# Expert attention: query, key and value projections as matmuls of 256 columns, and the PSUM tiles of the stage regrouped

## The chip, the core and the metric

The kernel runs on one core of a Trainium2 chip. A core has a matrix engine (PE, with its weight loads listed apart as PEld), a vector engine (DVE), a scalar engine (ACT), GpSimd (POOL) and an engine that issues DMAs (SP). Each runs its own queue of instructions in order; they wait for each other through semaphores. PE writes its results to PSUM, a small memory of eight banks of 512 float32 per partition; DVE and ACT read it from there. The metric is the time of one execution in device microseconds (us).

Before the change the median of 3 runs is 2612.46 us (2608.49 to 2620.51).

## The reference

A small vision model on 128 images, everything in float32: a tokenizer of two convolutions gives each image 64 tokens of 256 features; layer 0 has an attention with a ReLU distance, and then "expert attention"; layer 1 has a linear attention and a routed mixture of experts. The change is in expert attention alone. What that computes, cut to its core:

```python
xn = (x - mean) / sqrt(var + EPS) * norm_w
gate = softmax(xn @ router_w.T + router_b)             # 4 experts per token
xc = xn.reshape(B, T, C, DC)                           # C = 4 slices of DC = 64 features
qkv = einsum('btcd,ekd->btcek', xc, qkv_w)             # per slice and expert: q, k, v
q, k, v = ...                                          # H = 2 heads of 32 each
attn = softmax(einsum('bcehtd,bcehsd->bcehts', q, k) * scale)
y = einsum('bcehts,bcehsd->bcehtd', attn, v)
y = einsum('btced,eod->btceo', y, proj_w) + proj_b     # per expert
out = einsum('btceo,bte->btco', y, gate).reshape(B, T, D)
return residual + out @ out_w.T
```

An image has 64 tokens, so there are, for each image, 4 slices x 4 experts x 2 heads = 32 score matrices of 64 x 64.

## The kernel before

The stages follow each other: tokenizer (to 190 us in the trace), ReLU attention (to about 1085 us), expert attention (1085 to about 1824 us), then linear attention, routing and experts. In expert attention two images are worked on together, a **pair**, because 2 x 64 tokens fill the 128 partitions; there are 64 pairs, and four pairs form a block that shares statistics, transposes and gates. The order of work on every engine is written out by hand (`tc.manual_schedule()`): each engine executes its instructions in the order in which the Python code makes them. The framework puts in the semaphores, and gives each PSUM tile a slot of its pool; a slot is handed on when all who used its last tile are done.

`rest` (L1289) is the loop over pairs. One turn p works on three pairs at once: the scores and softmax of `cur` (pair p), the mixing of `old` (p-1), the output of `older` (p-2), and the projections of `new` (p+1). In order:

1. `cur.scores` (L1055, matmul L1064): 64 matmuls of 32 rows x 64 columns into two PSUM tiles of two banks (pool `fps`, tag `sc`). Then DVE: `maxima` (L1074) and `less_max` (L1078), two each.
2. `old.transposes` (L1100) and `transposed` (L1105): 16 transposes of the attention weights into four PSUM tiles of one bank (`pt`), each copied to SBUF by ACT.
3. Work for a later block (`do((p, "PE"))` and so on): in turns p%4 = 0 and 1 transposes of its normalised rows (`ptx`, L936, copied by ACT in L941), in p%4 = 2 the router's logits (L956), in p%4 = 3 the gates' softmax: DVE L976 to L978, ACT L981, DVE L984 and L985.
4. `older.output` (L1131, PSUM tile `po`), `old.mixed` (L1115, 32 matmuls, PSUM tile `pz`).
5. ACT: `cur.exponents` (L1081), two. DVE: `sums(0)` (L1084, L1085), then `older.added` (L1135), which adds `po` to the residual. POOL: `weights` (L1091, L1092).
6. ACT: `old.mixed_copied` (L1126), which copies `pz`.
7. `new.queries_keys(fc)` (L1004, matmul L1019), for the two halves fc of the features: 16 matmuls of 64 rows x 128 columns into a tile of tag `sc`, and after each half two copies by ACT (`queries_keys_copied`, L1025).
8. DVE: `cur.sums(1)`; POOL: `cur.weights(1)`.
9. `new.values(h)` for h = 1 and 0 (L1027, matmul L1039): 16 matmuls each, into two PSUM tiles of one bank (`pv`). `values_kept(h)` (L1047) takes them out: for h = 1 DVE adds the bias (L1053, two instructions), for h = 0 ACT copies (L1051, two).
10. `do((p, "DVE"))`: in turns p%4 = 1 and 2 statistics of later rows (L868, L869).

A float32 matmul is two MATMUL and two LDWEIGHTS rows in the trace, a transpose one of each. `pt`, `ptx`, `po`, `pz` and `pv` all come from one pool of four single banks (`apq`, tag `pq`, function `ps`, L303 to L306), in turn; the two tiles of tag `sc` take the other four banks.

Of the kernel before, what the change touches and what calls it, by code (L numbers as in the profile page):

```python
# [12 lines left out]
F32 = mybir.dt.float32  # L13
# [7 lines left out]
P = 128  # L21
# [38 lines left out]
def bcast(ap, axis, n):  # L60

    v = ap.unsqueeze(axis)
    shape = list(v.shape)
    shape[axis] = n
    return v.to_broadcast(shape)
# [225 lines left out]
class Shared:  # L291
# [3 lines left out]
    def __init__(self, c, ctx, end):  # L295
        def pool(name, bufs, ctx=ctx, **k):
            return ctx.enter_context(c.tc.tile_pool(name=name, bufs=bufs, **k))

        self.np_, self.bp, self.small = pool("an", 2), pool("ab", 2), pool("as", 1)

        self.atp, self.ep = (pool(n, k, end, side="right") for n, k in (("aat", 1), ("ae", 2)))
        self.end = end
        self.psq = pool("apq", 4, space=PSUM)  # L303

    def ps(self, shape, name):
        return self.psq.tile(shape, F32, tag="pq", name=name)  # L306
# [455 lines left out]
def expert_attention(c, sh, front, hd, normw, wr, br, wqkv, wvT, wproj, bproj, wout):  # L762
# [5 lines left out]
    SCALE = float(1.0 / np.sqrt(np.float32(32)))  # L768
    NP = B // 2
    NB = 4  # L770
    ps, small = sh.ps, sh.small
    nw = small.tile([P, 2], F32, name="nw")
    nc.sync.dma_start(nw, normw)
    wrs = small.tile([P, 2, 4], F32, name="wrs")
# [215 lines left out]
    class Pair:  # L990
# [10 lines left out]
            qk = ring(sh.bp, "k", [P, 2, 16, T])  # L1001
            self.qk = qk.rearrange("p (c a e t) -> p c a e t", c=4, a=2, e=2)

        def queries_keys(self, fc, among_scores=False):  # L1004

            if among_scores:
                pq = self.pools.pss.tile([P, 2, 2, 2, P], F32, tag="sc", name="pqk")
                pq = [pq[:, par] for par in range(2)]
            else:
                pq = [ps([P, 2, 2, P], "pqk") for _ in range(2)]  # L1010
            self.pq[fc] = pq
            for k in range(2):
                for eh in range(2):
                    for half in range(2):
                        o = slice(half * 64, half * 64 + 64)
                        for par in range(2):
                            r = slice(par * 64, par * 64 + 64)
                            f = k * D + eh * P + half * 64
                            nc.tensor.matmul(  # L1019
                                pq[par][o, k, eh, :], wt.w[r, f : f + 64], self.xT[r, fc], start=True, stop=True  # L1020
                            )

        def queries_keys_copied(self, fc, copy=nc.scalar.copy, pars=range(2)):
            for par in pars:
                copy(self.qk[:, 2 * fc + par], self.pq[fc][par])  # L1025

        def values(self, h):  # L1027

# [65 lines left out]
        def transposes(self, x, h):  # L1094

            e = self.e[x]
            self.pt[x, h] = pt = ps([P, 4, P], "pt")
            for cq in range(4):
                i = h * 8 + cq * 2
                nc.tensor.transpose(pt[:, cq, :], e[:, i : i + 2, :].rearrange("p e s -> p (e s)"), c.ident)  # L1100

        def transposed(self, x, h):
            if h == 0:
                self.pT[x] = self.pools.ep.tile([P, 2, 4, P], F32, tag="pT", name="pT")
            nc.scalar.copy(self.pT[x][:, h], self.pt.pop((x, h)))  # L1105

        def mixed(self):

            pz = ps([P, 2, P], "pz")
            for fc in range(2):  # L1110
                for j in range(2):
                    t = slice(j * 64, j * 64 + 64)
                    for r in range(4):
                        for par in range(2):
                            nc.tensor.matmul(  # L1115
                                pz[par * 64 : par * 64 + 64, fc, t],
                                self.v[:, par, r % 2, 2 * fc + j, r // 2 * 64 : r // 2 * 64 + 64],
                                self.pT[r // 2][:, r % 2, 2 * fc + par, t],
                                start=(r == 0),
                                stop=(r == 3),  # L1120
                            )
            self.pz = pz
# [3 lines left out]
            nc.scalar.copy(self.z, self.pz)  # L1126

        def output(self):
            self.po = po = ps([P, D], "po")
            for fc in range(2):  # L1130
                nc.tensor.matmul(po, self.z[:, fc], wt.o[:, fc, :], start=(fc == 0), stop=(fc == 1))  # L1131

# [56 lines left out]
    def do(key):  # L1189
        for step in work.pop(key, ()):  # L1190
            step()
# [46 lines left out]
    def first(cur, new, chunk, last):  # L1238

        new.queries_keys(0)  # L1240
        chunk.exponents()
        new.queries_keys_copied(0)
        chunk.sums()
        chunk.weights()
        cur.scores()
        cur.maxima(0)
        cur.less_max(0)
        y.normal_scalar(0)
        new.queries_keys(1)
        cur.maxima(1)  # L1250
        cur.less_max(1)
        chunk.transpose()
        new.queries_keys_copied(1)
        chunk.transposed()
        cur.exponents(0)
        last.outcome(0)
        last.outcome(1)
        for par in range(2):
            last.outcome_copied(0, par)
        cur.sums(0)  # L1260
        cur.weights(0)
        cur.exponents(1)
        for par in range(2):
            last.outcome_copied(1, par, nc.vector.tensor_copy)
        cur.sums(1)
        cur.weights(1)
        new.values(0)
        new.values_kept(0)
        last.back(0)
        last.back(1)  # L1270
        last.added(0)
        last.added(1)
        for k in range(1, 4):
            y.normal_scalar(k)
        new.values(1)
        new.values_kept(1)
        last.back(2)
        last.back(3)
        last.added(2)
        last.added(3)  # L1280
        sh.end.close()
        front.open()
        for k in range(NB):
            x.stream(k)
        do((0, "POOL"))
        do((0, "PE"))
        do((0, "ACT"))

    def rest(chunk, last):  # L1289
        with (  # L1290
            tc.tile_pool(name="fe", bufs=4) as ep,
            tc.tile_pool(name="fps", bufs=2, space=PSUM) as pss,
            tc.manual_schedule(),
        ):
            Pair.pools = SimpleNamespace(ep=ep, pss=pss)
            older, old, cur = None, None, pairs[0]
            for p in range(NP):
                new = Pair(p + 1, blocks[(p + 1) // NB]) if p + 1 < NP else None
                if p == 0:
                    first(cur, new, chunk, last)  # L1300
                    old, cur = cur, new
                    continue
                if p == 8:
                    front.weights()
                cur.scores()
                for x in range(2):
                    cur.maxima(x)
                for x in range(2):
                    cur.less_max(x)
                for x in range(2):  # L1310
                    for h in range(2):
                        old.transposes(x, h)
                        old.transposed(x, h)
                do((p, "PE"))
                do((p, "ACT"))
                do((p, "DVE0"))
                if older:
                    older.output()
                old.mixed()
                cur.exponents(0)  # L1320
                cur.exponents(1)
                do((p, "ACT1"))
                do((p, "DVE1"))
                do((p, "POOL0"))
                cur.sums(0)
                cur.weights(0)
                if older:
                    older.added()
                old.mixed_copied()
                if new:  # L1330
                    for fc in range(2):
                        new.queries_keys(fc, True)
                        new.queries_keys_copied(fc)
                else:
                    c.busy(ps([P, 2 * D], "idle"), wt.w, 3)
                do((p, "ACT2"))
                cur.sums(1)
                cur.weights(1, nc.gpsimd if new else nc.vector)
                do((p, "POOL"))
                if new:  # L1340
                    for h in (1, 0):
                        new.values(h)
                        new.values_kept(h)
                do((p, "DVE"))
                older, old, cur = old, cur, new
            for x in range(2):
                for h in range(2):
                    old.transposes(x, h)
                    old.transposed(x, h)
            older.output()  # L1350
            old.mixed()
            old.mixed_copied()
            older.added()
            old.output()
            old.added()
        assert not work
# [1004 lines left out]
```

## Time and profile before

| | us |
|---|---|
| median of 3 runs | 2612.46 |
| the profiled execution's own time | 2610.73 |
| its span in the trace, first to last instruction | 2609.0 |
| expert attention's scores, start of pair 1's to start of pair 63's | 702.8 (62 turns, 11.34 each) |

Busy time in stretches of that stage, in us:

| stretch | PE | DVE | ACT | POOL |
|---|---|---|---|---|
| 1100 to 1200 | 95.67 | 86.55 | 71.72 | 70.71 |
| 1400 to 1500 | 97.79 | 88.27 | 72.07 | 66.25 |
| 1600 to 1700 | 93.15 | 83.14 | 68.61 | 64.59 |

The granted clock of the matrix engine is 0.98 to 1.00 of full speed in these stretches. In the profile's lines a name such as `kr<-pqk` means that the instruction writes tile `kr` and reads `pqk`; several SBUF tiles have names of the buffers that they reuse (`kr` holds queries and keys, `vr` values, `xnr`, `xTr` and `oTr` normalised rows and weights). "x64" counts rows merged into one line; the time is from the first's start to the last's end. In square brackets stands how long the engine had been idle before, and which instruction's end released it.

### The profile page before, as it was taken

How to read it: one execution, taken by the hardware profiler on the slowest of the kernel's cores; microseconds unless marked ns; L12 is line 12 of the kernel's file. 1: busy time of each engine (PE TensorE's matmuls, PEld its weight loads, DVE VectorE, ACT ScalarE, POOL GpSimd, SP SyncE). 2: the span in 40 equal slices, each digit the busy share in tenths (PEclk: the TensorE clock that was granted, in tenths of full speed). 3: DMA queues.
4: the chain of work that ended last, by engine and by line, in shares of the span. 5: the costliest groups of instructions: out<-in, count | busy, mean ns of one | idle time of the engine just before them, and what ended most of it. 6: DMA issues, size and time to landing. Idle time of an engine off the chain costs nothing. (4 is left out here: it accounts for less than half of the span.)

```text
span 2609.0 us, 86024 instructions
## 1 busy us (share of the span) xinstructions
PE 2474.7 (95%) x37681; PEld 1702.5 (65%) x37681; DVE 2011.4 (77%) x3000; ACT 1635.0 (63%) x3421; POOL 1625.8 (62%) x1428
## 2 busy tenths in 40 slices
PE   8989999999999999899999999999999968999997
PEld 4554444444444444588888888887566557888886
DVE  5759999999999999888888888877567785444443
ACT  2228899898898888776667776675444533223232
POOL 3419989899898999676667676653233313454543
PEclk9999999999999999999999999999999989999998
DMA  3100000000000000000000000000344444555554
GB/s 112 36 13 1 2 2 2 2 2 2 2 2 1 2 13 2 3 29 14 24 14 24 15 24 15 14 24 24 82 96 99 94 118 175 191 189 190 191 193 133
DMA packets 138063, 141.47 MB, mean 54 GB/s; under 512 B 108001, under 2 KB 121859, under 8 KB 129870
## 3 DMA queue, kind: packets, MB, share of 16 engines
q1 hardware_dynamic: 128684, 119.48, 15.3%
q0 software_dynamic: 7648, 14.77, 1.8%
q8 instruction: 298, 4.88, 0.8%
q10 hardware_dynamic: 1344, 1.61, 0.2%
q14 instruction: 89, 0.73, 0.1%
HBM read 104.00 MB, written 32.54 MB: 52 GB/s over the span
## 5 line engine op out<-in xcount | busy, mean ns | idle before, releaser
L540 POOL TENSOR_TENSOR m<-q,k 128x1024 f32<-128x1024 f32 x384 | 719.9, 1910 | 55.9 <-PE sc L342 46.6
L532 DVE TENSOR_TENSOR m<-pc,k 128x2048 f32<-128x2048 f32 (+1 forms) x320 | 646.5, 2056 | 0.5 <-ACT q L472 0.5
L342 PE MATMUL sc<-m,wide 128*32 128x512 f32 x4096 | 520.1, 597 | 8.9 <-ACT m L541 6.6
L541 ACT ACTIVATE m<-m 128x1024 f32<-128x1024 f32 x384 | 402.6, 1049 | 20.6 <-POOL m L540 20.6
L342 PEld LDWEIGHTS sc<-m,wide 128*32 128x32 f32 x4096 | 134.7, 109 | 269.4 <-issue 157.2
L550 ACT ACTIVATE m<-k,q 128x64 f32<-128x64 f32 x1024 | 270.8, 339 | 0.9 <-DVE k L419 0.9
L1092 POOL TENSOR_TENSOR e<-e,mx 128x1024 f32<-128x1024 f32 x127 | 241.8, 1904 | 10.0
L1105 ACT COPY pT<-pt 128x512 f32<-128x512 f32 x256 | 133.9, 596 | 113.5 <-PE pt L1100 113.5
L2187 PE MATMUL ph<-xt,w1s 128*128 128x256 f32 x896 | 200.4, 382 | 1.8 <-DVE xt L2178 1.1
L2203 PE MATMUL po<-w2s,hT 128*128 128x256 f32 x896 | 198.0, 379 | 0.0
L1074 DVE TENSOR_REDUCE mx<-sc 128x16 f32<-128x1024 f32 x128 | 151.2, 1220 | 58.4 <-PE sc L1064 58.1
L2187 PEld LDWEIGHTS ph<-xt,w1s 128*128 128x128 f32 x896 | 171.1, 191 | 26.7 <-DVE xt L2178 1.8
L2203 PEld LDWEIGHTS po<-w2s,hT 128*128 128x128 f32 x896 | 168.1, 190 | 21.7
L2221 POOL DMA_INDIRECT out<-y,rout x56 | 56.6, 1011 | 168.1 <-ACT hT L2191 125.1
L1084 DVE TENSOR_REDUCE mx<-e 128x16 f32<-128x1024 f32 x128 | 154.7, 1209 | 8.6 <-ACT e L1081 6.7
L2191 ACT ACTIVATE hT<-ph,w1s 128x256 f32<-128x256 f32 x224 | 93.2, 471 | 98.6 <-PE ph L2187 98.6
L1081 ACT ACTIVATE e<-e 128x1024 f32<-128x1024 f32 x128 | 134.2, 1059 | 29.4 <-DVE e L1078 25.6
L1078 DVE TENSOR_TENSOR e<-sc,mx 128x1024 f32<-128x1024 f32 x128 | 150.2, 1214 | 0.1
L2208 ACT ACTIVATE y<-y,gf 128x256 f32<-128x256 f32 x56 | 28.0, 506 | 194.3 <-issue 106.9
L1025 ACT COPY kr<-pqk 128x512 f32<-128x512 f32 x254 | 130.5, 600 | 26.8 <-PE pqk L1019 26.7
L1100 PE MATMUL pt<-ident,e 128*128 128x128 f32 x1024 | 133.8, 283 | 9.6 <-POOL e L1092 3.7
L1115 PEld LDWEIGHTS pz<-pT,vr 128*64 128x64 f32 x4096 | 124.9, 138 | 21.9 <-ACT pT L1105 11.4
(337 smaller groups left out, 4850.5 us busy)
## 6 DMA issues: line engine op xcount, KB each, us to landing
w1s<-in_we SPq DMA_DIRECT2D x30, 1028.0 KB, 5.1
w2s<-in_we SPq DMA_DIRECT2D x30, 1024.0 KB, 4.9
h<-hd SPq DMA_DIRECT2D x4, 2048.0 KB, 12.0
hx<-h SPq DMA_DIRECT2D x4, 2048.0 KB, 12.3
out<-h SPq DMA_DIRECT2D x4, 2048.0 KB, 20.4
xt<-in_x SPq DMA_DIRECT2D x15, 512.0 KB, 3.6
hd<-h SPq DMA_DIRECT2D x15, 512.0 KB, 3.8
x<-hd SPq DMA_DIRECT2D x12, 512.0 KB, 3.6
```

The lines of the kernel that those rows point to most:

```text
L342: nc.tensor.matmul(dst[j : j + 32], wide[:, hf, s : s + 32], part, start=start, stop=stop)
L532: nc.vector.tensor_tensor(m, bcast(self.pq[:, hf, i : i + n], 3, T), k, ALU.max)
L540: nc.gpsimd.tensor_tensor(m, bcast(self.q[:, hf, s : s + 2], 3, T), k, ALU.subtract)
L541: nc.scalar.activation(m, m, AF.Relu)
L550: nc.scalar.activation(self.parts[i, hf][:, q], self.blk.k[:, hf, i], AF.Relu, bias=self.q[:, hf, i - NB // 2, q : q + 1], scale=-1.0,)
L1074: nc.vector.tensor_reduce(mx, self.sc[x].rearrange("p h c s -> p (h c) s"), AX.X, ALU.max)
L1078: nc.vector.tensor_sub(e, self.sc[x].rearrange("p h c s -> p (h c) s"), bcast(self.sm[x], 2, T))
L1081: nc.scalar.activation(self.e[x], self.e[x], AF.Exp, scale=SCALE)
L1084: nc.vector.tensor_reduce(self.sm[x], self.e[x], AX.X, ALU.add)
L1092: eng.tensor_mul(e, e, bcast(sm, 2, T))
L2187: nc.tensor.matmul(ph[:, j], self.w1[:, w0 : w0 + P], self.xt[:, fc], start=(fc == 0), stop=(fc == 1))
L2203: nc.tensor.matmul(po, self.hT[:, f, r * P : r * P + P], self.w2[:, f, :], start=(f == 0), stop=(f == 7))
```

## The change

Queries and keys: `all_queries_keys` takes the place of two calls of `queries_keys`. A matmul now streams both halves fc at once, 256 columns in place of 128, so there are 16 where there were 32. Each PSUM tile (tag `sc`) belongs to one `par` and holds both fc. All 16 matmuls stand ahead of the four copies by ACT.

Values: `all_values` takes the place of two calls of `values`. A matmul streams both halves h at once, 256 columns, 16 in place of 32. There are two PSUM tiles `pv` of two banks, one per `par`; h = 0 lies in columns 0 to 127 of each group of 256, h = 1 in the others, so each bank holds parts of both. ACT copies the h = 0 columns and DVE adds the bias to the h = 1 columns of the same tile.

PSUM: after the first turn the pool of four single banks is closed, and a pool of two tiles of two banks (`fpq`) opened. `pt` has one tile per x for both h. A tile `pom` ("room") has `po` and `pz` in its first bank, and what `ps` gave to the work for a later block (`ptx`, logits, gates) in its second. In a turn the slots are taken in this order: `pt`, `pt`, `pom`, `pv`, `pv`.

```diff
+    def ps(shape, name):
+        if room.pool is None:
+            return sh.ps(shape, name)
+        n = int(np.prod(shape[1:]))
+        t = room.other[: shape[0], :n]
+        return t if len(shape) == 2 else t.rearrange("p (a b) -> p a b", a=shape[1])
+
+    def new_room():
+        t = room.pool.tile([P, 2, 512], F32, tag="pq", name="pom")
+        room.mixing, room.other = t[:, 0], t[:, 1]
...
+        def all_queries_keys(self):
+            self.pq = [self.pools.pss.tile([P, 2, 2, 2, P], F32, tag="sc", name="pqk") for _ in range(2)]
+            for k in range(2):
+                for eh in range(2):
+                    for half in range(2):
+                        o = slice(half * 64, half * 64 + 64)
+                        for par in range(2):
+                            r = slice(par * 64, par * 64 + 64)
+                            f = k * D + eh * P + half * 64
+                            nc.tensor.matmul(
+                                self.pq[par][o, k, eh], wt.w[r, f : f + 64], self.xT[r], start=True, stop=True
+                            )
+
+        def all_queries_keys_copied(self):
+            for par in range(2):
+                for fc in range(2):
+                    nc.scalar.copy(self.qk[:, 2 * fc + par], self.pq[par][:, :, :, fc])
+
+        def all_values(self):
+            v = ring(sh.bp, "v", [P, 8, D])
+            self.v = v.rearrange("p (a h m n) -> p a h m n", a=2, h=2, m=4)
+            self.pv = [room.pool.tile([P, 4, D], F32, tag="pq", name="pv") for _ in range(2)]
+            for fc in range(2):
+                for j in range(2):
+                    for eh in range(2):
+                        for par in range(2):
+                            r = slice(par * 64, par * 64 + 64)
+                            nc.tensor.matmul(
+                                self.pv[par][eh * 64 : eh * 64 + 64, 2 * fc + j, :],
+                                self.xT[r, fc, j * 64 : j * 64 + 64],
+                                wt.vp[r, eh, :],
+                                start=True,
+                                stop=True,
+                            )
+
+        def all_values_kept(self):
+            for par in range(2):
+                nc.scalar.copy(self.v[:, par, 0], self.pv[par][:, :, 0:P])
+                nc.vector.tensor_add(self.v[:, par, 1], self.pv[par][:, :, P:D], bcast(wt.b, 1, 4))
...
-            self.pt[x, h] = pt = ps([P, 4, P], "pt")
+            if h == 0:
+                self.pt[x] = room.pool.tile([P, 2, 4, P], F32, tag="pq", name="pt")
+            pt = self.pt[x][:, h]
...
-            pz = ps([P, 2, P], "pz")
+            pz = room.mixing[:, D : 2 * D].rearrange("p (c t) -> p c t", c=2)
...
-            self.po = po = ps([P, D], "po")
+            self.po = po = room.mixing[:, 0:D]
...
                     first(cur, new, chunk, last)
+                    sh.pq.close()
+                    room.pool = late.enter_context(tc.tile_pool(name="fpq", bufs=2, space=PSUM))
...
                         old.transposed(x, h)
+                new_room()
                 do((p, "PE"))
...
-                    for fc in range(2):
-                        new.queries_keys(fc, True)
-                        new.queries_keys_copied(fc)
+                    new.all_queries_keys()
+                    new.all_queries_keys_copied()
...
-                    for h in (1, 0):
-                        new.values(h)
-                        new.values_kept(h)
+                    new.all_values()
+                    new.all_values_kept()
```

The first turn (`first`) keeps the old forms, since it shares its time with the end of ReLU attention.

## The prediction

> **What bounds the kernel now.** I read the shares of busy time first, then the timeline of one steady turn, engine by engine, then who waits at the scores. The page's first rows:
>
> ```profile
> PE 2474.7 (95%) x37681; PEld 1702.5 (65%) x37681; DVE 2011.4 (77%) x3000; ACT 1635.0 (63%) x3421; POOL 1625.8 (62%) x1428
> ```
>
> PE is nearly full, in expert attention too. The timeline of PE for the turn that begins at 1511.55 (one with p%4 = 1):
>
> ```profile
> 1511.55 1.97 PE L1100 MATMUL pt<-ident,e 128*128 128x128 f32 x16
> 1513.35 0.60 PE L936 MATMUL ptx<-ident,xTr 128*128 128x128 f32 x4
> 1513.79 1.03 PE L1131 MATMUL po<-xTr,z 128*128 128x256 f32 x4
> 1514.75 2.09 PE L1115 MATMUL pz<-pT,vr 128*64 128x64 f32 x64
> 1516.76 1.98 PE L1019 MATMUL pqk<-xnr,xTr 64*64 64x128 f32 x64
> 1518.56 1.93 PE L1039 MATMUL pv<-xTr,xnr 64*64 64x128 f32 x64
> 1520.42 1.84 PE L1064 MATMUL sc<-kr 32*64 32x64 f32 x128
> ```
>
> Each group starts as the one before runs out: no wait for another engine. The same turn on ACT and DVE:
>
> ```profile
> 1517.33 0.35 ACT L1126 COPY z<-pz 128x256 f32<-128x256 f32 x1
> 1517.99 2.05 ACT L1025 COPY kr<-pqk 128x512 f32<-128x512 f32 x4 [0.30 <-PE pqk L1019]
> 1520.59 1.07 ACT L1051 COPY vr<-pv 128x512 f32<-128x512 f32 x2 [0.55 <-PE pv L1039]
> ```
>
> ```profile
> 1511.66 2.36 DVE L1074 TENSOR_REDUCE mx<-sc 128x16 f32<-128x1024 f32 x2 [1.09 <-PE sc L1064]
> ...
> 1517.75 0.36 DVE L1135 TENSOR_TENSOR h<-h,po 128x256 f32<-128x256 f32 x1
> 1518.03 1.21 DVE L1084 TENSOR_REDUCE mx<-e 128x16 f32<-128x1024 f32 x1
> 1519.27 0.25 DVE L1085 RECIPROCAL mx<-mx 128x16 f32<-128x16 f32 x1
> 1519.66 1.29 DVE L1053 TENSOR_TENSOR vr<-pv,xTr 128x512 f32<-128x512 f32 x2
> 1520.87 0.42 DVE L868 BATCH_NORM_STATS2 st<-h 128x6 f32<-128x256 f32 x1
> ...
> 1522.29 1.22 DVE L1074 TENSOR_REDUCE mx<-sc 128x16 f32<-128x1024 f32 x1 [0.19 <-PE sc L1064]
> ```
>
> See three things: `z` is copied before DVE adds `po` (1517.33 against 1517.75); ACT copies `pqk` while PE's second half runs; DVE is done with `pv` (1520.95) while ACT still copies its own part. DVE, with statistics, is in time for the next scores by 0.19 only. DVE and ACT are not the bound, but their slack is thin.
>
> A turn is 10.39 from scores to scores where nothing halts PE (several turns have just that); the mean is 11.34. Most of the difference is PE standing still with nothing to wait for:
>
> ```profile
> L1064 PE MATMUL sc<-kr 32*64 32x64 f32 x8192 | 110.7, 232 | 26.6 <-issue 25.5 <-DVE e L568 0.9
> ```
>
> Counted over PE's rows, these stops stand 256 instructions of PE apart (762 rows for three, with a few unlisted ones), and the instruction queue moves packets of 16 KB, 256 instructions: it is code arriving late. A block of 256 that ends in a stop lasted 2.7 to 3.9 us; I take 3.1 as the time that a block needs. Stops of over 100 ns sum to about 42 us between 1102 and 1807, 0.69 per turn.
>
> **The matmuls themselves: no gain on the array.** Starts of single MATMUL rows in the 64 of `pqk` come in fours, 107 ns from four to four: 64 x 107 / 4 = 1.71 us, which is what first start to last start measures. An `output` row of 256 columns follows the next after 216 ns on the full array, so 128 columns are 107: four quarters of the array stream without a hole. 32 rows of twice the columns, four at a time, take 8 x 214 = 1.71. The block stays at 1.80 with its change-over. [...]
>
> **Fewer instructions: some stops go.** A turn has 128 fewer rows of PE (64 MATMUL, 64 LDWEIGHTS). 256 rows of scores take 1.5 us, 5.9 ns each; a row of `pv` takes 14 ns now, 27 after. If a block ends x rows into the scores, it lasted 5.9x + 14(256-x) ns before: under 3.1 us from x = 62 on, a mean stop of 0.6, about as measured (0.69 with the transposes behind). After: under 3.1 from x = 180, and from about 205 when the scores also start 0.5 late (below): 0.1, and 0.1 behind the scores: 0.2 per turn. This alone would be worth 0.5 x 62 = 30 us.
>
> **Queries and keys: copies come later.** Before, ACT started its four copies 1.23 us after PE began the block (0.85 of half a block and 0.38 until ACT starts). Now each `par` is complete only at the end: 1.71 + 0.38 = 2.09. Call ACT's first copy c. Copies end at c + 2.05; the next scores need both `sc` slots, so start at c + 2.07. Before, scores followed `pv`, 3.66 after the block's begin; now 2.09 + 2.07 = 4.16. PE loses 0.5 a turn.
>
> **One room for `ptx`, `po`, `pz`.** Its slot comes from `pt` of x = 0: both copies must be done. The second ended at 1513.38, PE went on at 1513.35: 0.1 lost. Turn p%4 = 0 or 1 by PE: 10.39 + 0.5 + 0.1 = 11.0.
>
> **A bank read by two engines.** This is the step that decides. `po` and `pz` share a bank, and each bank of `pv` is read by ACT and DVE. [...] The trace shows such ordering: in ReLU attention `pc` is read by both, and
>
> ```profile
> who waited for it (us, times):
> ...
>   DVE m L532: 0.5, 1
> ```
>
> stands under ACT's copy of `pc` (L472), whose own output DVE's L532 doesn't read; DVE waits on ACT's semaphore in every chunk. If reads are ordered by bank as in the code: (a) `z` waits for DVE's add; (b) DVE's part of `pv` waits for ACT's, tile by tile. Let M be the start of DVE's first maximum.
>
> (a) The add ends 6.45 after M (1518.11 - 1511.66); 0.09 to wake ACT (as from `less_max` to `exponents`), `z` takes 0.35 with 0.1 overlapped by the next copy: c is M + 6.8 at the earliest. In the turn with gates the add ends 7.96 after M (1497.48 - 1489.52): c = M + 8.3.
>
> (b) `pv` on PE must wait for the room's slot, free when `z` is copied: c + 0.15. ACT's first `pv` copy comes 2.03 after `pv` begins (1520.59 - 1518.56), c + 2.18. It ends at c + 2.8, the second at c + 3.3; DVE's adds then run c + 2.9 to 3.5 and 3.5 to 4.1. Next M = c + 4.1, or c + 5.3 behind statistics (1.2); the scores alone would allow c + 3.7.
>
> From c to c, the four turns: p%4 = 0 and 1 (no statistics in the turn before): 4.1 + 6.8 = 10.9, under PE's 11.0, so **11.0** each; 2: 5.3 + 6.8 = **12.1**; 3: 5.3 + 8.3 = **13.6**. Sum 47.7; stops of 0.2 show in the two PE-bound ones, hidden in the others: 48.1. Before: 4 x 11.34 = 45.3. So +2.8 for each of 15.5 groups of four: **+43 us**. Queued behind the waiting `z` are ACT's six copies, and behind those PE's scores; behind DVE's adds stand statistics and the maxima. POOL's weights are ready by M + 10.6, before the transposes need them. No DMA changes.
>
> Against the profiled execution's own 2610.73 this is 2654; that execution is 1.7 below the median of 2612.46, within the runs' spread.
>
> **Rivals.** *Faster, 2597*: the two orders of (a) and (b) are not made, or by address only, and fewer code stops decide. Then PE bounds: 11.0, 11.0, 11.0 and 11.2 and at least 0.2 of stops are 44.4, -0.9 per four, -14 us. For it: 42 us of stops are real. Against it: the wait on `pc`. It decides if the ordering costs under 0.9 per four. *No change, 2606*: only one of the orders bites: without (a), DVE has 0.7 to spare before c is late, PE's 44.2 and 0.8 of stops are 45.0, -5. *Slower, but less, 2636*: (a) without (b): M comes by the scores, c + 3.7 or 4.7 behind statistics; 11.0 + 11.0 + 11.5 + 13.0 + 0.4 = 46.9, +25. [...]
>
> **Numbers.** Both orders: 0.62. (a) alone: 0.14. No change: 0.10. Faster: 0.14. A measurement of this kernel tells about 0.5% from no change. Faster 0.14, within 0.10, slower 0.76. The likeliest case's own range: stops hidden wholly (-6), wake-ups 0.1 shorter at three places (-5 to -10), stops not reduced (+15), wake-ups longer by as much at two of them (+6): 2638 to 2675. The range for 8 in 10 reaches down to the faster case: 2597 to 2675.
>
> **What would show it.** Right: ACT idle ahead of `z` released by DVE L1135; DVE idle ahead of its `pv` add released by ACT's `vr` copy; PE idle ahead of scores for ACT's `kr` or of `pv` for `z`; turns p%4 = 3 the longest; PE's busy share down. Code stops: less idle on "issue" at the scores. The matmuls: `pqk` as 32 MATMUL rows in 1.7 us. Wrong: DVE and ACT on `pv` at once; `z` ahead of the add; or blocks of `pqk` well under 1.7.

## The result, and the profile after

| | us |
|---|---|
| changed kernel, median of 4 runs | 2811.51 (2804.05 to 2813.3) |
| kernel before, median of 4 runs (the three from above and one more) | 2610.47 (2607.83 to 2620.51) |
| ratio | 1.0757, 95% interval 1.0722 to 1.0792 |
| span of the profiled executions, before and after | 2609.0 and 2809.5 |
| start of pair 1's scores to start of pair 63's, before and after | 702.8 and 895.1 (11.34 and 14.44 a turn) |

The change costs about 200 us, and 192 of them lie in 62 turns of expert attention's loop. The forecast was 43. The page's first row and one of its costliest groups say that PE now stands idle:

```profile
PE 2534.3 (90%) x33713; PEld 1651.0 (59%) x33713; DVE 2015.0 (72%) x3000; ACT 1640.3 (58%) x3421; POOL 1628.7 (58%) x1428
...
L1154 PE MATMUL pt<-ident,e 128*128 128x128 f32 x1024 | 154.5, 284 | 97.2 <-ACT pT L1159 93.7
```

The same group on the page of the kernel before:

```profile
L1100 PE MATMUL pt<-ident,e 128*128 128x128 f32 x1024 | 133.8, 283 | 9.6 <-POOL e L1092 3.7
```

There are 3968 matmul rows fewer than the 37681 before (64 in each of 62 turns), and PE's share fell from 95 to 90%. PE stood idle ahead of the transposes `pt` for 9.6 us in the kernel before and for 97.2 now, nearly all of it waiting for ACT's copies `pT`. The timeline of PE for a turn without gates (p%4 = 0) of the changed kernel:

```profile
1613.58 0.66 PE L1154 MATMUL pt<-ident,e 128*128 128x128 f32 x4
1614.97 1.09 PE L1154 MATMUL pt<-ident,e 128*128 128x128 f32 x8 [0.73 <-ACT pT L1159]
1616.79 0.66 PE L1154 MATMUL pt<-ident,e 128*128 128x128 f32 x4 [0.73 <-ACT pT L1159]
1617.28 0.60 PE L951 MATMUL pom<-ident,xTr 128*128 128x128 f32 x4
1618.71 1.13 PE L1185 MATMUL pom<-xTr,z 128*128 128x256 f32 x4 [0.83 <-ACT xTr L956]
1619.77 2.09 PE L1169 MATMUL pom<-pT,vr 128*64 128x64 f32 x64
1621.79 1.96 PE L1047 MATMUL pqk<-xnr,xTr 64*64 64x256 f32 x32
1623.56 1.91 PE L1066 MATMUL pv<-xTr,xnr 64*64 64x256 f32 x32
...
1625.95 1.53 PE L1116 MATMUL sc<-kr 32*64 32x64 f32 x120 [0.21 <-ACT kr L1054]
```

From 1613.58 to the next such start, 1627.41, are 13.83 us, where 10.39 were possible before. Start by start: `pt` 3.70 in place of 1.80 (**+1.90**, two halts of 0.73 and the restarts); `ptx` to `po` 1.43 in place of 0.44 (**+0.99**: output waits until ACT has read `ptx`); scores 2.01 in place of 1.52 (**+0.49**). That is 3.38 of the 3.44 us that this turn is longer. The blocks of `pqk` and `pv` are as long as before, 1.77 and 1.84 from start to start, with half as many rows. A turn with gates (p%4 = 3):

```profile
1600.57 0.29 PE L986 MATMUL pom<-ident,lg 128*128 128x16 f32 x2
1603.33 1.13 PE L1185 MATMUL pom<-xTr,z 128*128 128x256 f32 x4 [2.46 <-DVE gate L993]
1604.39 3.64 PE L1169 MATMUL pom<-pT,vr 128*64 128x64 f32 x64
1607.95 1.96 PE L1047 MATMUL pqk<-xnr,xTr 64*64 64x256 f32 x32
```

Here output waits 2.46 us for DVE's L993, which reads the gates' logits in the *second* bank of `pom`; output writes the first. And the same 64 rows of `mixed` last 3.64 in place of 2.09: PE was granted 0.50 of its clock from 1604.48 to 1607.89 (more on this in the last section). The waits of the whole stage after (who waited for whom, then us in total, times, longest):

```profile
PEld pt L1154 <- ACT pT L1159: 120.1, 124, 1.2
...
DVE vr L1077 <- ACT vr L1076: 169.3, 62, 3.8
ACT z L1180 <- DVE h L1189: 146.8, 62, 5.6
...
PE pom L1185 <- DVE gate L993: 34.9, 15, 2.6
```

124 halts inside `pt` are two in each of 62 turns. `z` behind DVE's add and DVE's `pv` adds behind ACT's copies, 62 times each, are the prediction's steps (a) and (b). Turns p%4 = 0, 1, 2 and 3 last 13.83, 13.83, 13.53 and 16.68 (medians, scores to scores); the prediction had 11.0, 11.0, 12.1 and 13.6, without stops for code.

### The profile page after: what moved, and what is told of

Read it like the earlier page. It is cut to its first block, busy times and chain, and to the rows that moved or that the text cites. A ratio compares the mean times of both kernels' runs of the same rounds, so it can differ in the third digit from the quotient of the medians.

```text
span 2809.5 us, 78104 instructions
## 1 busy us (share of the span) xinstructions
PE 2534.3 (90%) x33713; PEld 1651.0 (59%) x33713; DVE 2015.0 (72%) x3000; ACT 1640.3 (58%) x3421; POOL 1628.7 (58%) x1428
## 3 DMA queue, kind: packets, MB, share of 16 engines
q8 instruction: 267, 4.37, 0.6%
## 5 line engine op out<-in xcount | busy, mean ns | idle before, releaser
L1159 ACT COPY pT<-pt 128x512 f32<-128x512 f32 x256 | 144.1, 586 | 182.6 <-PE pt L1154 182.4
L1154 PE MATMUL pt<-ident,e 128*128 128x128 f32 x1024 | 154.5, 284 | 97.2 <-ACT pT L1159 93.7
L1143 POOL TENSOR_TENSOR mx<-mx,gate 128x16 f32<-128x16 f32 x127 | 27.6, 217 | 342.2 <-DVE mx L1137 303.5
L1077 DVE TENSOR_TENSOR vr<-pv,xTr 128x512 f32<-128x512 f32 x124 | 79.8, 686 | 169.3 <-ACT vr L1076 169.3
L1154 PEld LDWEIGHTS pt<-ident,e 128*128 128x128 f32 x1024 | 109.0, 141 | 132.4 <-ACT pT L1159 124.0
L1169 PEld LDWEIGHTS pom<-pT,vr 128*64 128x64 f32 x4096 | 139.5, 151 | 24.9 <-issue 23.8
```

## The experiments

Two theories stood against each other for the part that nobody had forecast. **W**: the semaphores order a PSUM tile as a whole between engines, whatever bank an access touches. **B**: accesses are ordered by bank, and PE's new halts come from the hand-over of the slots from one tile to the next.

**One part of the changed kernel undone at a time.** pt_together changes only the order in which the program states the work; every engine still has the same instructions in the same order:

```diff
...
                     for h in range(2):
                         old.transposes(x, h)
+                    for h in range(2):
                         old.transposed(x, h)
```

> The changed kernel with both halves' transposes of an x placed ahead of both copies; each engine's own order stays. Theory W (a PSUM tile is ordered as a whole between engines, whatever bank an access touches): both waits of PE for pT inside pt (0.73 us each, 1.9 us of a turn's transposes with the restart) go; the turn falls from 13.8 to about 12.0, the time from 2811 to about 2695 (2680 to 2725). Theory B (ordered by bank; the waits come from the slots' hand-over): nothing moves, 2800 to 2820.

Measured: 2755.11, ratio to before 1.0553 (1.0532 to 1.0573), 56 us less than the changed kernel. PE's timeline of a gates' turn of pt_together:

```profile
1511.15 1.97 PE L1154 MATMUL pt<-ident,e 128*128 128x128 f32 x16
1513.46 0.40 PE L986 MATMUL pom<-ident,lg 128*128 128x16 f32 x2 [0.34 <-ACT pT L1159]
1517.61 1.42 PE L1185 MATMUL pom<-xTr,z 128*128 128x256 f32 x4 [3.75 <-DVE gate L993]
```

The 16 transposes run as one group of 1.97 again: both halts are gone, without any slot or bank moved. That rules out B for these halts. The time, though, is 30 us above W's range: of the 116 us that W expected, 60 are missing. Turns without gates fell only to 12.2 to 12.6; and the gates' turn stayed at 16.73, since what PE gained at `pt` it lost at output (3.75 in place of 2.46).

other_apart gives the work for a later block a tile of its own:

```diff
-        t = room.pool.tile([P, 2, 512], F32, tag="pq", name="pom")
-        room.mixing, room.other = t[:, 0], t[:, 1]
+        t = room.pool.tile([P, 2, 512], F32, tag="pq", name="pot")
+        u = room.pool.tile([P, 2, 512], F32, tag="pq", name="pom")
+        room.mixing, room.other = u[:, 0], t[:, 0]
```

> The changed kernel with the work for a later block (ptx, logits, gates) in a tile of its own, so six tiles of two banks a turn in place of five. Theory W: output no longer waits for ACT's copy of ptx (about 0.8 us) or, in the gates' turn, for DVE's softmax input (2.5 us); but po's tile now takes the slot of the second pt, so it waits for the last pT copy (about 0.7). Turns without gates stay at 13.5 to 13.8, the gates' turn falls from 16.7 to about 14.5; time about 2775 (2755 to 2800). Theory B: the wait for L993 is no matter of the tile and stays; 2800 to 2825.

Measured: 2740.72, 1.0486 (1.0461 to 1.0511), 71 us less than the changed kernel, where W expected 36 and at most 56. The gates' turn of other_apart:

```profile
1516.74 0.29 PE L987 MATMUL pot<-ident,lg 128*128 128x16 f32 x2
1517.58 1.13 PE L1186 MATMUL pom<-xTr,z 128*128 128x256 f32 x4 [0.54 <-ACT pT L1160]
1518.64 2.09 PE L1170 MATMUL pom<-pT,vr 128*64 128x64 f32 x64
```

Output no longer waits for DVE's L993, though DVE still executes it at the same place: the wait was the tile's. It waits 0.54 for the slot instead. And `mixed` is back at 2.09. The gates' turn fell from 16.68 to 13.64. The stretches of half clock fell too, from 61.4 us in the stage to 23.9 (mean granted clock of the profiled executions 0.977 and 0.983); at half rate, that is up to 19 of the 71 us (an estimate from these lengths). The waits of both runs say W; both of its sizes were off.

both_apart joins the two.

> pt_together and other_apart in one: what is left of the change are the late copies of pqk, the shared bank of po and pz, and pv shared by ACT and DVE. This is what the prediction priced, but for po's slot, which now waits for the last pT copy (about 0.5 a turn in place of 0.1). Theory W (a tile is ordered as a whole, and that was the only thing missing in the prediction): turns of 11.5, 11.5, 12.1 and 13.6, with stops 49.1 per four against 45.3 before: about 2667 (2645 to 2695). If another cost is hidden in the change, 2700 or more.

Measured: 2685.0, 1.0261 (1.024 to 1.0283), 126.5 less than the changed kernel: the two parts add up (56 and 71). The turns last 11.57, 11.99, 12.21 and 13.43 (medians). The last two come near the prediction's 12.1 and 13.6; the first two are 0.6 and 1.0 longer than its 11.0, where PE waits for `pT` at `ptx` and at `po`, for the slots.

z_first takes step (a) out:

```diff
-                if older:
-                    older.added()
                 old.mixed_copied()
+                if older:
+                    older.added()
```

> both_apart with ACT's copy of pz made ahead of DVE's add of po in the program, so that the add waits for z and not z for the add. If the prediction's step (a) holds: ACT's idle time ahead of z for DVE goes, the gates' turn falls from 13.6 to under 12, about 2.5 us less per four turns: 2632 (2615 to 2655). If z's wait was covered: as both_apart.

Measured: 2675.15, 1.0222 (1.0197 to 1.0247): 10 less than both_apart, where 35 were expected. ACT no longer waits for DVE ahead of `z`, but the scores still wait for `kr`, and PE for the slots:

```profile
1511.02 0.64 PE L972 MATMUL pot<-xnr,xTr 128*32 128x128 f32 x16 [0.35 <-ACT pT L1160]
1512.00 1.13 PE L1186 MATMUL pom<-xTr,z 128*128 128x256 f32 x4 [0.34 <-ACT pT L1160]
...
1519.24 1.53 PE L1117 MATMUL sc<-kr 32*64 32x64 f32 x120 [0.21 <-ACT kr L1055]
```

repaired also cuts the projections' tiles so that the first of two is complete after half of its block (its copies are changed to match):

```diff
-                                self.pq[par][o, k, eh], wt.w[r, f : f + 64], self.xT[r], start=True, stop=True
+                                self.pq[k][o, par, eh], wt.w[r, f : f + 64], self.xT[r], start=True, stop=True
...
-                                self.pv[par][eh * 64 : eh * 64 + 64, 2 * fc + j, :],
+                                self.pv[fc][eh * 64 : eh * 64 + 64, par, j, :],
```

> z_first, and the projections' tiles cut so that each is complete after half of its block: pqk by query and key, pv by half fc, ACT and DVE each on a tile in turn. The copies of pqk start 0.86 earlier, DVE's adds of pv about 1.5 earlier. PE's scores no longer wait for kr; left is po's wait for the last pT copy, 0.5 a turn, and few stops: about 10.39 + 0.5 + 0.2 = 11.1, 2598 (2580 to 2620).

Measured: 2644.58, 1.0115 (1.0093 to 1.0137), still above before and 47 above what was expected. The scores' halt is gone from the timeline; what is left are waits for the slots of two banks, here both in a gates' turn of repaired:

```profile
1508.80 0.40 PE L987 MATMUL pot<-ident,lg 128*128 128x16 f32 x2 [0.34 <-ACT pT L1164]
1509.78 1.13 PE L1190 MATMUL pom<-xTr,z 128*128 128x256 f32 x4 [0.58 <-ACT pT L1164]
```

Over the 62 turns, PE's waits for `pT` at these two places sum to 45 us, more than the 31 that repaired lacks to before. They were not taken out by themselves, so that they are the whole rest is not shown. The run v256_qk_by_k below, with the same wide matmuls and the old single banks, is 56 us faster than repaired: the regrouping of PSUM loses more than the wide matmuls gain, even with the orders mended.

**The parts added to the kernel before, one at a time.** qk256_alone has only the query and key matmuls of the change (`all_queries_keys` and its copies).

> The kernel before with only the query and key matmuls at 256 columns (tiles of the scores' tag as in the change; pool of four single banks and values as before). The copies start 0.86 us later and scores about 0.5 late; stops for code shrink by about 0.3 of 0.69 a turn: +12 us, 2622 (2605 to 2645). [...]

Measured: 2618.03, 1.0028 (1.0014 to 1.0041): slightly slower. ACT's idle time ahead of `kr` and PE's ahead of the scores show the late copies; the block of `pqk` took 1.78 from start to start (1521.74 to 1523.52), against 1.80 in the kernel before:

```profile
1512.97 2.05 ACT L1044 COPY kr<-pqk 128x512 f32<-128x512 f32 x4 [1.52 <-PE pqk L1037]
```

```profile
1515.07 1.53 PE L1083 MATMUL sc<-kr 32*64 32x64 f32 x120 [0.19 <-ACT kr L1044]
...
1521.74 1.96 PE L1037 MATMUL pqk<-xnr,xTr 64*64 64x256 f32 x32
1523.52 1.93 PE L1058 MATMUL pv<-xTr,xnr 64*64 64x128 f32 x64
```

v256_alone has only the value matmuls at 256 columns, in tiles of one bank, each filled by four matmuls:

```diff
+            for fc in range(2):
+                for par in range(2):
+                    self.pv[par, fc] = ps([P, 2, D], "pv")
...
+                for par in range(2):
+                    m = slice(2 * fc, 2 * fc + 2)
+                    nc.scalar.copy(self.v[:, par, 0, m], self.pv[par, fc][:, :, 0:P])
+                    nc.vector.tensor_add(self.v[:, par, 1, m], self.pv[par, fc][:, :, P:D], bcast(wt.b, 1, 2))
```

> The kernel before with only the value matmuls at 256 columns, each tile one bank for one par and one half fc, ACT and DVE each taking 128 of every 256 columns of each tile (8 instructions of half the size in place of 4). Stops for code fall from 0.69 to about 0.35 a turn, nothing is later: about -20 us, 2590 (2580 to 2612). If ordering two readers of one tile costs by itself: DVE idle for ACT's vr, and 2612 or more.

Measured: 2594.3, 0.9928 (0.9906 to 0.995): faster than before. DVE does wait for ACT on each tile, but a tile is a quarter of the whole and the first two are ready at half of the block:

```profile
1514.85 1.41 DVE L1049 TENSOR_TENSOR vr<-pv,xTr 128x256 f32<-128x256 f32 x4 [0.83 <-ACT vr L1048]
```

v256_qk_by_k adds the query and key matmuls with one tile for queries and one for keys, as in repaired.

> v256_alone with the query and key matmuls at 256 columns too, the tiles by query and key, so that ACT's first two copies run beside the second half of the block as before. 64 more rows of PE go; the stops that v256_alone has left lie in blocks that are nearly all scores, so little more is to be had: 2590 (2580 to 2598). If the later copies still cost (as in qk256_alone, +10): 2600 or more.

Measured: 2588.75, 0.99 (0.9881 to 0.9918): 1% faster than before, and faster than the changed kernel. Over these four blocks PE has no wait; earlier in the same turn, inside `pt`, it has one of 0.52 for POOL:

```profile
1497.04 1.96 PE L1061 MATMUL pqk<-xnr,xTr 64*64 64x256 f32 x32
1498.82 1.91 PE L1039 MATMUL pv<-xTr,xnr 64*64 64x256 f32 x32
1500.65 1.59 PE L1108 MATMUL sc<-kr 32*64 32x64 f32 x128
1502.18 1.97 PE L1144 MATMUL pt<-ident,e 128*128 128x128 f32 x16
```

po_pz_shared has nothing of the change but the shared bank of `po` and `pz`, on the kernel before.

> The kernel before with po and pz in one tile of one bank, as the change has them, and nothing else. The prediction's step (a) alone: z waits for DVE's add. Turns without gates have some 0.3 to spare (z would be copied at 6.8 after the maxima's start, pqk's first copy comes at 6.4 to 6.9); in the gates' turn z is about 2 us later and holds ACT's six copies. About +1.5 per four turns, 2633 (2618 to 2655); ACT idle ahead of z for DVE in all turns. If (a) is covered by other waits: 2612 (2600 to 2618).

> po_pz_shared with ACT's copy of pz made ahead of DVE's add in the program. The add then waits for z, which is ready when PE's block pz is; DVE loses at most 0.3 where it was early. 2612 (2600 to 2622) if the order of the two is all that step (a) costs; as po_pz_shared if it is the sharing itself.

Measured: po_pz_shared 2625.11, 1.0051 (1.0034 to 1.0068); po_pz_z_first 2616.52, 1.0022 (1.0011 to 1.0033). The waits of po_pz_shared hold the step, 61 times, and those of po_pz_z_first have no such row:

```profile
ACT z L1131 <- DVE h L1140: 72.0, 61, 2.2
```

So (a) costs 15 us on the kernel before. Turning the order round wins 9 of them back, and 6 stay. The 15 fall short of the 23 us (1.5 per four turns) that the prediction's arithmetic gave.

## Why the prediction was wrong

The sign was right, and the size was 43 where 201 were measured: most of the cost came from a step that was priced at almost nothing. By the prediction's own steps:

- **"No gain on the array."** Right. At full clock 32 rows of 256 columns take the time of 64 of 128 in the turns shown (1.77 and 1.78 against 1.80).
- **"Fewer instructions: some stops go."** Right in kind. In the stage before, 46 gaps of over 100 ns stand at one and the same place of every 256 rows of PE and PEld, semaphore rows counted in. From row to row they sum to 42.6 us, where no other place has more than 1.8. At that place stand 22.9 us in qk256_alone, 16.9 in v256_alone and 8.6 in v256_qk_by_k. Forecast for the change were 12. The changed kernel has 7.4 there, but other places have up to 8.2, so its stops can't be told from its other halts; in both_apart, where PE halts less, they are 18.8. The queue that moves instructions (q8 on the pages) has 298 packets with 4.88 MB before and 267 with 4.37 after: 31 packets of 16 KB fewer for 7936 rows of PE and PEld fewer, 256 a packet. The 36 longest of the 46 stops, those over 300 ns, each end 1.19 to 1.51 us after the end of such a packet. These stops are what the wide matmuls can win: v256_qk_by_k has 34 us less of them and is 25 faster in the median (half clock, 13.7 us before and none there, is at most 7 of the 25).
- **"Copies come later."** Right in kind: 0.49 a turn measured against 0.5. With the stops won back it made qk256_alone 10 us slower (expected ahead of the run: 12).
- **"A bank read by two engines", (a) and (b).** Both waits are there, in each of 62 turns: 146.8 us ahead of `z` and 169.3 ahead of the `pv` adds. In each of them the two readers share a tile; that two reads of one bank have to be ordered where the tiles differ, no run shows. (b) was not undone by itself, so its cost stays open. The size of (a) was too large: 15 us on the kernel before, and 10 from both_apart to z_first.
- **"One room for ptx, po, pz ... 0.1 lost."** This is the step that failed. It asked only when the slot of `pom` becomes free. It took for granted that accesses to different banks of one tile don't wait for each other: `pt`'s two halves, one bank each, were given no cost, and `pom`'s two banks none. The runs showed the tile to be the unit: 1.90 a turn at `pt`, with two halts inside it (pt_together removes them), and 0.99, or a wait of 2.46 in the gates' turn, at output (other_apart removes it). Together they are 126.5 us, both_apart against the changed kernel, the clock's part included.
- With these two taken out, both_apart is 2685.0, 31 above the forecast of 2654. Part of this is a second, smaller miss in the same step: in pt_together, with the change's own five tiles, PE waits 0.34 a turn at the slot of `pom` (21 us in 62 turns), not 0.1. Part belongs to the experiment: with a sixth tile, `po` waits for the last copy of `pt` as well, and the waits for slots come to 0.71 a turn (44 us). And the stops for code are 18.8 us in place of 12.
- **The rivals.** None held the size, and that a tile is ordered as a whole was not among them. The prediction's evidence, the wait on `pc` in ReLU attention, could not tell bank from tile: that `pc` has 264 float32 and lies in one bank. The trace of before had a place that could. In the tokenizer `pc` has 1024 float32, two banks; ACT's L196 reads a part of the first, and the last of PE's matmuls (L184) write the second:

```profile
L196 ACT ACTIVATE y<-pc x32: 384/384/385, 23.3 to 178.4; 128x256 f32<-128x256 f32 x32
...
its engine sat idle before it (us, times) until:
  PE pc L184: 90.7, 38
```

All 48 executions of L196 start 0.05 or 0.10 us after the end of the last matmul; by then the first bank had been complete for 0.9 us or more. That is what W says. The cost of the new tiles should have been worked out for both cases.

## What to carry to other kernels

When small PSUM tiles are merged into larger ones, list for each new tile every engine that touches any part of it, in program order; each change of engine in that list can be a halt unless other work lies between (in the changed kernel 0.73 us each inside `pt`, 0.83 and 2.46 ahead of output). Sharing tiles cost far more here (126.5 us) than the smaller number of matmuls was worth (25 us), and stating all writes of a tile ahead of all its reads removed the halts inside `pt` without moving a single instruction on any engine. The gain of the wider matmuls here came with fewer stops for code, and it is kept when tiles are cut so that they are complete early, as in v256_qk_by_k.

## What the runs showed of the hardware

PE's halts went together with a lower clock. The changed kernel's trace has 14 stretches of half clock in the stage, 61.4 us in all; before has 4 with 13.7, both_apart 4 with 17.1, v256_qk_by_k none. The mean granted clocks of these profiled executions are 0.977, 0.985, 0.984 and 0.987. The halts at output count most: pt_together, without the halts inside `pt` but with longer ones at output, still has 68.3 us (mean clock 0.976), and other_apart, with the halts inside `pt` but not the gates' one, 23.9 (0.983). In two stretches of a gates' turn of the changed kernel (columns: stretch, length, then busy time and rows of PE, PEld, DVE, ACT and POOL, granted clock, DMA share, GB/s):

```profile
1658.70:1665.20 6.50, 2.61 (x32) 1.97 (x19) 6.34 (x12) 3.75 (x6) 1.23 (x1) 1.00 0.01 3
1665.20:1669.90 4.70, 4.67 (x72) 3.92 (x75) 1.71 (x4) 0.72 (x2) 2.17 (x3) 0.64 0.02 5
```

PE was busy for 2.61 of 6.50 us, and in the next 4.7 us it got 0.64 of its clock: output and `mixed` took 4.6 us from start to the next block's start (1665.23 to 1669.83), where a turn without gates took 3.08. So the halt of 2.46 us was followed by 1.5 us more in the same turn.

The starts of the 14 stretches in the changed kernel's trace lie whole multiples of 3.41 us apart; ten of them last 3.41 us and four 6.83, all at 0.50 of the clock. In the 3.41 us ahead of each the granted clock was 1.00, and PE was busy for 0.79 to 1.67 us, 23 to 49% of the time. How little work it takes for the clock to fall was not shown.

How many of the 201 us this is was not measured by itself; the 48 us more at half clock bound it at about 24 (an estimate from the lengths above).
